# Four combinations on VectorE, moved in between the sums of the fourth weight piece

## The chip, the cores and the metric

The kernel runs on one core of one Trainium2 chip. The metric is the device time of one execution in microseconds (us). Five engines matter: TensorE (PE; PEld is its weight load), VectorE (DVE), ScalarE (ACT), GpSimd (POOL) and SyncE (SP), which issues most of the transfers (DMAs).

## The reference

The input `x` has the shape (32, 128, 2048). Two layers of the same form follow each other: `x = x + ffn(cond(x))`. Cut to what matters here, the first layer is

```python
out = einsum('boi,bih->boh', agg_w, x) + agg_b      # cond: one 128 x 128 mix for each batch
out = einsum('bsd,od->bso', out, W) + bias          # ffn: 2048 x 2048
xa  = einsum('bsd,erd->ebsr', out, A)               # 16 low-rank updates of rank 16
upd = einsum('ebsr,eor,e->bso', xa, Bf, coeffs * scales)
```

The second layer is a grouped convolution with 9 taps, and an up and a down projection with a GELU between them on permuted columns.

The 16 low-rank updates have together the rank 256, so the kernel folds them into the weights: W' = W^T + A^T diag(coeffs x scales) B^T. W' is 2048 x 2048; A and B^T have 256 rows, which are two halves of 128 (called `c` in the code).

## The kernel before

**The large product.** `x` times W' is computed by Strassen's scheme on two levels. The outer level has seven rounds (`ROUNDS`: P1, P2, P6, P7, P5, P3, P4), and each round runs over NG = 8 groups of four batches. `multiply` does one group of one round; it holds the seven inner products, each of four matmuls of 128 x 128 by 128 x 512 (L332). The inner combinations of the weights are made on GpSimd by `inner_weights` (L239 to L243), those of `x` by `x_combine` (L296 to L299). The second layer's work is put between the products of the last round, and the two projections (L676, L687) end the kernel.

**Building W'.** W' is made in 16 blocks (`blocks`), each of four pieces of 128 x 512, with two indices kh and oh for the quarter and kc for the place in it. The first four blocks (kh = oh = 0) are made directly by `w_make`, one after the other: for each piece two matmuls over the two halves `c` (L172), into a bank of PSUM, and a sum on VectorE that adds the bank to W^T's piece in SBUF (L176). The other twelve blocks are made two at a time by `w_make_two`, in front of each of the first six groups of the first round. That function uses Strassen's scheme too: seven products of one matmul for each block (L210), each followed on VectorE by a sum into a piece of W' (L213). P1, P6, P7 and P4 of a block accumulate in one bank, and the sum behind each of them reads it, so the next of them waits for that sum. The products take combinations of A's columns (`a_combine`, on GpSimd, L184 to L187) and of B^T's columns (`b_combine`): four subtractions of 128 x 512 (L196 to L199), the second of which uses the first and the fourth the second. `tb[1]` serves the blocks with oh = 1 and is made on VectorE; `tb[0]` is made on GpSimd in a later group. P1 and P2 need no combination of B^T, P6 needs the second.

**The order.** The order of instructions on each engine is written out by hand: it is that in which the Python code calls them (`manual_schedule`), and each engine takes its own instructions in that order. Buffers come from one pool of 24 slots (`slot`), and eight banks of PSUM go round in a queue (`bank`, `done`). The opening order is: loads of A, of B^T for oh = 0, of the first blocks of W^T; then of B^T for oh = 1 (`b_load(1, q)`, L141, into `bf_sb[1]`) and of the fifth and sixth block (L156); `a_combine(0)`; the four direct blocks by `make_first` from within `inner_weights`; `b_combine(1)`; then the loop over the steps, whose first iteration issues `w_make_two` for the fifth and sixth block and then `multiply`. `make_first` also adds a piece of each block to `wsum` on GpSimd (L870), the sums over W' from which a later bias is made.

In `b_combine` the four source pieces are those of the two halves and two column groups:

```python
b11, b12, b21, b22 = (bf_sb[oh][:, c, oi] for c in range(2) for oi in range(2))
```

Of the kernel before, what the change touches and what calls it, by code (L numbers as in the profile page):

```python
# [11 lines left out]
ALU = mybir.AluOpType  # L12
# [39 lines left out]
def adaln_ffn_kernel(  # L52
# [16 lines left out]
    nc = tc.nc  # L69
# [8 lines left out]
    def slot(name, shape=(P, L)):  # L78
        return big.tile(list(shape), FP, name=name, tag="s")


    def bank():
        return banks.pop(0)

    def done(*ps):
        banks.extend(ps)
# [39 lines left out]
    def a_load(h, k0, k1):  # L126
        for ki in range(2):
            i0 = (2 * h + ki) * QW
            nc.sync.dma_start(
                a_sb[h][:, :, ki, k0:k1].rearrange("p c k i -> p c (k i)"),  # L130
                A[:, :, i0 + k0 * P : i0 + k1 * P],
            )
# [26 lines left out]
    def w_store(k, t):  # L159
        nc.gpsimd.dma_start(wb_d[k], t.rearrange("p k o c -> p (k o c)"))  # L160

    def w_make(k, t):

        kh, oh, kc = k
        for oi in range(2):
            for ki in range(2):
                pw = bank()

                n = QW // 2 if k == (0, 0, 0) and oi == 0 else QW
                for o0 in range(0, QW, n):  # L170
                    for c in range(2):
                        nc.tensor.matmul(  # L172
                            pw[:, o0 : o0 + n], lhsT=a_sb[kh][:, c, ki, kc],
                            rhs=bf_sb[oh][:, c, oi, o0 : o0 + n], start=(c == 0), stop=(c == 1),
                        )
                nc.vector.tensor_tensor(t[:, ki, oi], pw, t[:, ki, oi], ALU.add)  # L176
                done(pw)
        w_store(k, t)


# [12 lines left out]
    def b_combine(oh, tt):  # L193
        t = slot(f"tb_{oh}", (P, 4, QW))
        b11, b12, b21, b22 = (bf_sb[oh][:, c, oi] for c in range(2) for oi in range(2))
        tt(t[:, 0], b12, b11, ALU.subtract)  # L196
        tt(t[:, 1], b22, t[:, 0], ALU.subtract)
        tt(t[:, 2], b22, b12, ALU.subtract)
        tt(t[:, 3], b21, t[:, 1], ALU.subtract)  # L199
        return {  # L200
            "P1": b11, "P2": b21, "P3": b22, "P4": t[:, 3],
            "P5": t[:, 0], "P6": t[:, 1], "P7": t[:, 2],
        }
# [67 lines left out]
    def x_loads(r, g):  # L271
        return {
            "P1": lambda: [x_load(g, 0, 0)],
            "P2": lambda: [x_load(g, 0, 1)],
            "P6": lambda: [x_load(g, 1, 0), x_load(g, 1, 1), x_load(g, 0, 0)],
            "P7": lambda: [x_load(g, 0, 0), x_load(g, 1, 0)],
            "P5": lambda: [x_load(g, 1, 0), x_load(g, 1, 1)],
            "P4": lambda: [x_load(g, 1, 1)],
            "P3": lambda: [x_load(g, 0, 1), part_load("s2", g)],
        }[r]()  # L280

    def x_combine(r, g, ts):

        a = ts[0]
        tt = nc.gpsimd.tensor_tensor
        if r == "P6":

            b, a, c = ts
            pieces(b, b, a, ALU.add)
            pieces(a, b, c, ALU.subtract)  # L290
            part_store("s2", g, a)
        if r in ("P7", "P5", "P3"):
            pieces(a, a, ts[1], ALU.add if r == "P5" else ALU.subtract)
        s = slot(f"s_{r}{g}", (P, 4, QW))
        a11, a12, a21, a22 = a[:, 0, 0], a[:, 1, 0], a[:, 0, 1], a[:, 1, 1]
        tt(s[:, 0], a21, a22, ALU.add)  # L296
        tt(s[:, 1], s[:, 0], a11, ALU.subtract)
        tt(s[:, 2], a11, a21, ALU.subtract)
        tt(s[:, 3], a12, s[:, 1], ALU.subtract)  # L299
        return {  # L300
            "P1": a11, "P2": a12, "P3": s[:, 3], "P4": a22,
            "P5": s[:, 0], "P6": s[:, 1], "P7": s[:, 2],
        }
# [412 lines left out]
    def small():  # L716
# [120 lines left out]
    blocks = [  # L837
        (kh, oh, kc) for kh, oh in ((0, 0), (0, 1), (1, 1), (1, 0)) for kc in range(4)
    ]
# [20 lines left out]
    lhs, sa, tb = {}, {}, {}  # L860
    sa[0] = a_combine(0, nc.gpsimd.tensor_tensor)
    first = [wt.pop(k) for k in blocks[0:4]]

    def make_first(kc):
        t = first[kc]
        w_make(blocks[kc], t)
        made.append(blocks[kc])
        if kc == 2:
            lhs[0] = x_combine(*steps[0], xs.pop(0))
        nc.gpsimd.tensor_tensor(wsum[:, 0, 1], wsum[:, 0, 1], t[:, 0, 1], ALU.add)  # L870

    rhs = inner_weights("P1", first, make_first)
    tb[1] = b_combine(1, nc.vector.tensor_tensor)
    a_load(1, 0, 4)
    unsummed, unsummed_first = [], list(first)
    olds = {}
# [4 lines left out]
    def olds_load(i):  # L881
        r, g = steps[i]
        olds[i] = [old and part_load(old, g) for old, _ in ADDED[r]]

    for i, (r, g) in enumerate(steps):
        ri = i // NG
        last_round = ri + 1 == len(ROUNDS)
        if i + 1 < len(steps):
            if i + 1 not in xs:
                xs[i + 1] = x_loads(*steps[i + 1])  # L890
            if not last_round:
                lhs[i + 1] = x_combine(*steps[i + 1], xs.pop(i + 1))
        if i + 2 < len(steps) and ri > 0 and not last_round:
            xs[i + 2] = x_loads(*steps[i + 2])
        if i == 0:
            olds_load(0)
        if i + 1 < len(steps) and not last_round:
            olds_load(i + 1)
        if g == NG - (1 if ri else 2) and ri < len(ROUNDS) - 1:
            nxt = inner_weights(ROUNDS[ri + 1], [nxt[kc] for kc in range(4)])  # L900

        if ri == 0:
            ks = blocks[4 + 2 * g : 6 + 2 * g]
            if ks:
                two = [wt.pop(k) for k in ks]
                w_make_two(ks, two, sa[ks[0][0]], tb[ks[0][1]])
                made.extend(ks)
                if g == 1:
                    a_scale(1, 0, 4)
                    sa[1] = a_combine(1, nc.gpsimd.tensor_tensor)  # L910
                if g == 3:
                    tb[0] = b_combine(0, nc.gpsimd.tensor_tensor)
                for k, t in zip(ks, two):
                    unsummed.append((k[1], t))
                    if k[:2] == (1, 0):
                        nxt[k[2]] = t
        elif ri + 1 < len(ROUNDS):
            for k, combine in waiting.items():
                nxt[k] = combine()
            waiting = {}  # L920
            if 2 <= g < 6:
                waiting[g - 2] = outer_weights(ROUNDS[ri + 1], g - 2)

        if last_round and g == 0:
            late_loads()
        if last_round and g == 2:

            late["te"] = mix.rearrange("p (k r) c -> p k r c", k=2)
            nc.sync.dma_start(mix.rearrange("p k c -> p (k c)"), te_d)
        k0 = 3 * (g - NG)  # L930
        if last_round:
            stage(k0, stage_first)

        def between(j):
            b = (ri - 1) * (NG - 2) + g
            if ri > 0 and g < NG - 2 and b < B and j < KEXP // 2:
                mixed_kernel(b, (2 * j, 2 * j + 1))
            if ri == 0 and j == 2:
                for k in blocks[6 + 2 * g : 8 + 2 * g]:
                    wt[k] = w_load(*k)  # L940
            if ri == 0 and j in (1, 3) and unsummed:
                row_sums(*unsummed.pop())
            if ri == 0 and j == 5 and unsummed_first:
                t = unsummed_first.pop(0)
                tt = nc.vector.tensor_tensor
                tt(wsum[:, 0, 0], wsum[:, 0, 0], t[:, 0, 0], ALU.add)
                tt(wsum[:, 0], wsum[:, 0], t[:, 1], ALU.add)
            if last_round:
                if j == 3 and i + 1 < len(steps):
                    lhs[i + 1] = x_combine(*steps[i + 1], xs.pop(i + 1))  # L950
                    olds_load(i + 1)
                if j in (2, 4):
                    stage(k0 + j // 2, stage_first)
                if j % 2:
                    stage_third(k0 + j // 2)
                else:
                    stage(k0 + j // 2, stage_second)

        multiply(r, g, lhs.pop(i), rhs, olds.pop(i), between)
        next(chain, None)  # L960
        if last_round and g >= 6:
            pair(g - 6)
        if last_round and g == 7:
            rings()
            gather_two(0)
        if g == NG - 1 and ri + 1 < len(ROUNDS):
            rhs = nxt
            nxt = {}

    before = None  # L970
    for k, (g, h) in enumerate(heads):
# [5 lines left out]
        t = ts.pop(k)  # L977
# [75 lines left out]
```

## Time and profile before

| what | value |
|---|---|
| median of 3 runs | 2651.13 us (2650.91 to 2654.36) |
| the profiled execution, its own time | 2649.93 us |
| its span (first to last instruction) | 2648.2 us |
| TensorE busy in the span | 2620.2 us, 99% |
| VectorE busy | 1335.3 us, 50% |
| GpSimd busy | 1200.2 us, 45% |
| ScalarE busy | 535.2 us, 20% |
| TensorE's products of L210, share of the chain that ended last | 2% |
| TensorE's products of L332, share of that chain | 49% |

The times of the profile are microseconds from the start of the span. A group of instructions is named by its line, its engine, its operation and its tiles, with buffer numbers left out. "PE bank L210 <- DVE w L213" reads: TensorE's instruction of L210, which writes a bank, waited for VectorE's instruction of L213, which writes `w`. A float32 matmul appears as two records. Busy shares of an engine that is not the bound say little: what counts is which wait ends last at a place.

### The profile page before, as it was taken

What the parts mean: (1) busy time and instruction counts of PE and PEld (TensorE: products, weight loads), DVE (VectorE), ACT (ScalarE), POOL (GpSimd) and SP (SyncE); (2) the same over time, 40 slices, a digit from 0 to 9 for tenths busy, and PEclk for the clock granted to TensorE, in tenths of its full rate; (3) what the DMA queues carried; (4) which work ended last, traced back from release to release, by engine and by line L of the source; (5) the groups of instructions that cost most, each with busy time, mean ns of one, the idle gap of its engine ahead of it and who ended that gap; (6) DMA issues with size and microseconds to landing.
All of it is one profiled execution on the core that took longest, in us unless ns stands there. A gap on an engine that the chain in (4) does not pass through costs nothing.

```text
span 2648.2 us, 20100 instructions
## 1 busy us (share of the span) xinstructions
PE 2620.2 (99%) x6484; PEld 1234.3 (47%) x6484; DVE 1335.3 (50%) x2168; ACT 535.2 (20%) x1103; POOL 1200.2 (45%) x950
## 2 busy tenths in 40 slices
PE   9999999999999999999999999999999999999998
PEld 4444444444444444444444445555455544555543
DVE  5554134343233454433366666666666666666610
ACT  0000000000000000000011144444444444444432
POOL 7321536978756644756332333333433333333222
PEclk9999999999999999999999999999999999999999
DMA  8542458688466577565657788777678777777532
GB/s 317 201 163 103 163 194 325 266 327 351 153 247 254 221 284 288 222 256 201 226 203 240 221 304 283 234 220 232 228 248 255 224 227 227 239 240 237 164 126 88
DMA packets 183609, 609.18 MB, mean 230 GB/s; under 512 B 16848, under 2 KB 88016, under 8 KB 139088
## 3 DMA queue, kind: packets, MB, share of 16 engines
q1 hardware_dynamic: 150080, 474.79, 50.8%
q0 software_dynamic: 32992, 132.14, 14.5%
q8 instruction: 52, 0.85, 0.1%
q10 hardware_dynamic: 432, 0.96, 0.1%
q14 instruction: 53, 0.43, 0.0%
HBM read 372.42 MB, written 201.85 MB: 217 GB/s over the span
## 4 chain that ended last, share of the span: by engine, by line
PE 95%; DVE 2%; DMA 1%; issue 1%; SPq 0%; ACT 0%; POOLq 0%; DVEq 0%; ACTq 0%
PE bank L332 49%; PE bank L676 16%; PE bank L687 16%; PE bank L534 6%; PE bank L444 4%; PE bank L210 2%; PE bank L172 1%; DMA xg<-x 1%; DVE va L514 0%; DVE vb L513 0%; DVE vb L516 0%; DMA ws<-in_ffw 0%; DVE va L515 0%; DVE va L517 0%; DMA bf_sb<-in_BfT 0%
## 5 line engine op out<-in xcount | busy, mean ns | idle before, releaser
L676 PE MATMUL bank<-t,ws 128*128 128x512 f32 x1024 | 460.7, 593 | 1.0 <-DVE u L325 0.5
L687 PE MATMUL bank<-gl,ws 128*128 128x512 f32 x1024 | 460.2, 592 | 0.0
L694 POOL DMA_INDIRECT out<-t,orow x128 | 151.7, 1185 | 562.3 <-DVE t L692 493.8
L325 DVE TENSOR_TENSOR u<-bank,u 128x512 f32<-128x512 f32 x280 | 187.6, 688 | 418.0 <-PE bank L332 411.0
L679 ACT ACTIVATE gl<-bank 128x512 f32<-128x512 f32 x512 | 306.0, 598 | 447.3 <-PE bank L676 445.1
L332 PE MATMUL bank<-P_t,s_P 128*128 128x512 f32 x896 | 393.7, 592 | 0.0
L687 PEld LDWEIGHTS bank<-gl,ws 128*128 128x128 f32 x1024 | 194.8, 190 | 232.7 <-issue 230.8
L676 PEld LDWEIGHTS bank<-t,ws 128*128 128x128 f32 x1024 | 194.6, 190 | 228.0 <-issue 219.2
L332 PE MATMUL bank<-wo_P,s_P 128*128 128x512 f32 x640 | 283.1, 595 | 1.5 <-DVE u L325 1.5
L332 PE MATMUL bank<-wo_P,xt 128*128 128x512 f32 x640 | 281.5, 592 | 0.0
L332 PEld LDWEIGHTS bank<-P_t,s_P 128*128 128x128 f32 x896 | 170.5, 190 | 213.2 <-issue 211.2
L435 ACT ACTIVATE bank<-w,aggb 128x512 f32<-128x512 f32 x128 | 80.8, 684 | 890.2 <-DVE ags L406 872.6
L427 POOL TENSOR_TENSOR x<-x,fb 128x1024 f32<-128x1024 f32 x64 | 155.5, 2448 | 226.1 <-DMA x<-in_x 176.1
L692 DVE TENSOR_TENSOR t<-bank,t 128x512 f32<-128x512 f32 x128 | 87.9, 687 | 318.0 <-PE bank L687 318.0
L269 POOL TENSOR_TENSOR xt<-xt,xt 128x512 f32<-128x512 f32 x128 | 159.6, 1280 | 157.7 <-DMA xt<-in_xT 157.7
L332 PE MATMUL bank<-P_t,xt 128*128 128x512 f32 x448 | 201.5, 593 | 0.0
L325 DVE TENSOR_TENSOR p<-bank,p 128x512 f32<-128x512 f32 x112 | 77.5, 692 | 238.8 <-PE bank L332 238.8
L296 POOL TENSOR_TENSOR s_P<-xt 128x512 f32<-128x512 f32 x56 | 71.8, 1283 | 272.1 <-DMA xt<-in_xT 215.8
L332 PEld LDWEIGHTS bank<-wo_P,s_P 128*128 128x128 f32 x640 | 122.3, 191 | 154.2 <-issue 152.5
L332 PEld LDWEIGHTS bank<-wo_P,xt 128*128 128x128 f32 x640 | 121.7, 190 | 152.1 <-issue 150.1
L406 DVE SCALAR_TENSOR_TENSOR ags<-mix,att_bc,ags 128x128 f32<-128x128 f32 x224 | 155.9, 696 | 4.5
L660 POOL DMA_INDIRECT t<-hx_d,row x128 | 124.8, 975 | 59.9 <-issue 24.7
(144 smaller groups left out, 2649.6 us busy)
## 6 DMA issues: line engine op xcount, KB each, us to landing
xt<-in_xT SPq DMA_DIRECT2D x88, 1024.0 KB, 8.9
u<-u_d SPq DMA_DIRECT2D x40, 1024.0 KB, 11.3
wo_P<-wb_d SPq DMA_DIRECT2D x36, 1024.0 KB, 14.2
u<-c_d SPq DMA_DIRECT2D x64, 512.0 KB, 5.9
x<-in_x SPq DMA_DIRECT2D x32, 1024.0 KB, 8.0
xg<-x SPq DMA_DIRECT2D x256, 128.0 KB, 5.6
hx_d<-x1t SPq DMA_DIRECT2D x32, 1024.0 KB, 5.3
hx_d<-ht SPq DMA_DIRECT2D x32, 1024.0 KB, 7.0
```

Of the source, the lines that this page charges most:

```text
L269: nc.gpsimd.tensor_tensor(out[:, i, j], a[:, i, j], b[:, i, j], op)
L325: nc.vector.tensor_tensor(to, ps, to, ALU.add)
L332: nc.tensor.matmul(ps, lhsT=lhs[k][:, bass.ts(kc, P)], rhs=rhs[k][kc], start=first and kc == 0, stop=last and kc == 3, skip_group_check=True,)
L406: nc.vector.scalar_tensor_tensor(ag, mix[:, k], att, ag, ALU.mult, ALU.add)
L427: nc.gpsimd.tensor_tensor(xt[:, f : f + 2], xt[:, f : f + 2], late["fb"][:, f : f + 2], ALU.add)
L444: nc.tensor.matmul(pm, lhsT=ag, rhs=u[:, f], start=False, stop=True, skip_group_check=True)
L534: nc.tensor.matmul(out, lhsT=w[:, 2 * i + r], rhs=rhs, start=first and r == 0, stop=last and r == 1, skip_group_check=True,)
L660: nc.gpsimd.indirect_dma_start(out=t.rearrange("p k t -> p (k t)"), out_offset=None, in_=hx_d[g].rearrange("l k t -> l (k t)"), in_offset= ...
L676: nc.tensor.matmul(pu, lhsT=w[:, m * P : (m + 1) * P], rhs=t[:, 0], start=True, stop=True)
L679: nc.scalar.activation(gl[m], pu, AF.Gelu)
L687: nc.tensor.matmul(pd, lhsT=w[:, (MC + m) * P : (MC + m + 1) * P], rhs=gl[m], start=(m == 0), stop=(m == MC - 1),)
L694: nc.gpsimd.indirect_dma_start(out=out, out_offset=bass.IndirectOffsetOnAxis(ap=orow[:, g, h : h + 1], axis=0), in_=t[:, 1], in_offset=None,)
```

## The change

`b_combine` no longer issues its four subtractions. It allocates their buffer, and returns a function `part`, each call of which issues the next of the four, together with the table of operands. `w_make` takes a function `between` and calls it after each of its four sums; by default it does nothing. For the fourth direct block `make_first` hands it `part` of `b_combine(1)`, so VectorE gets sum, combination, sum, combination, sum, combination, sum, combination in place of four sums and then four combinations. The buffer for `tb[1]` is allocated ahead of `inner_weights` instead of behind it. For `tb[0]` the four calls of `part` stand in a loop at the old place.

```diff
-    def w_make(k, t):
+    def w_make(k, t, between=lambda: None):
...
                 nc.vector.tensor_tensor(t[:, ki, oi], pw, t[:, ki, oi], ALU.add)
                 done(pw)
+                between()
         w_store(k, t)
...
     def b_combine(oh, tt):
         t = slot(f"tb_{oh}", (P, 4, QW))
         b11, b12, b21, b22 = (bf_sb[oh][:, c, oi] for c in range(2) for oi in range(2))
-        tt(t[:, 0], b12, b11, ALU.subtract)
-        tt(t[:, 1], b22, t[:, 0], ALU.subtract)
-        tt(t[:, 2], b22, b12, ALU.subtract)
-        tt(t[:, 3], b21, t[:, 1], ALU.subtract)
-        return {
+        parts = [
+            (t[:, 0], b12, b11), (t[:, 1], b22, t[:, 0]), (t[:, 2], b22, b12), (t[:, 3], b21, t[:, 1])
+        ]
+
+        def part():
+            if parts:
+                tt(*parts.pop(0), ALU.subtract)
+
+        return part, {
             "P1": b11, "P2": b21, "P3": b22, "P4": t[:, 3],
             "P5": t[:, 0], "P6": t[:, 1], "P7": t[:, 2],
         }
...
     first = [wt.pop(k) for k in blocks[0:4]]
 
+    part, tb[1] = b_combine(1, nc.vector.tensor_tensor)
+
     def make_first(kc):
         t = first[kc]
-        w_make(blocks[kc], t)
+
+        if kc == 3:
+            w_make(blocks[kc], t, part)
+        else:
+            w_make(blocks[kc], t)
         made.append(blocks[kc])
...
     rhs = inner_weights("P1", first, make_first)
-    tb[1] = b_combine(1, nc.vector.tensor_tensor)
     a_load(1, 0, 4)
...
                 if g == 3:
-                    tb[0] = b_combine(0, nc.gpsimd.tensor_tensor)
+                    part, tb[0] = b_combine(0, nc.gpsimd.tensor_tensor)
+                    for _ in range(4):
+                        part()
```

## The prediction

> **What bounds the kernel now.** I read the busy shares first, then TensorE's waits in the opening stage, then the engines' own timelines around the longest of them.
>
> ```profile
> PE 2620.2 (99%) x6484; PEld 1234.3 (47%) x6484; DVE 1335.3 (50%) x2168; ACT 535.2 (20%) x1103; POOL 1200.2 (45%) x950
> PE bank L210 <- DVE w L213: 4.0, 1, 4.0
> ```
>
> TensorE is busy for all but 28 us of 2648.2 us, so only what shortens its idle time or its slow clock can move the end. The second line (waits of the first 62 us: who waited for whom, us in total, times, longest) is the longest single wait of the whole run: one wait of 4.0 us, in which TensorE stands before the products of L210 until VectorE has added a sum of L213. TensorE's timeline shows where (start, length, records; in brackets the idle time before):
>
> ```profile
> 35.51 3.60 PE L210 MATMUL bank<-bf_sb,a_sb 128*128 128x512 f32 x8
> 43.09 7.08 PE L210 MATMUL bank<-tb,sa 128*128 128x512 f32 x12 [3.98 <-DVE w L213]
> 50.01 1.88 PE L210 MATMUL bank<-bf_sb,sa 128*128 128x512 f32 x4
> ```
>
> One product here is two records, 0.43 us each at full clock (the four from 50.01 are followed at 51.73). The eight from 35.51 are P1 and P2 for the two weight blocks; the product P6 of the first block is then due at 38.95 and starts at 43.09. VectorE in the same time:
>
> ```profile
> 33.99 0.69 DVE L176 TENSOR_TENSOR w<-bank,w 128x512 f32<-128x512 f32 x1 [1.02 <-PE bank L172]
> 35.71 0.69 DVE L176 TENSOR_TENSOR w<-bank,w 128x512 f32<-128x512 f32 x1 [1.03 <-PE bank L172]
> 36.32 1.01 DVE L196 TENSOR_TENSOR tb<-bf_sb 128x512 f32<-128x512 f32 x1
> 37.37 1.64 DVE L197 TENSOR_TENSOR tb<-bf_sb,tb 128x512 f32<-128x512 f32 x1
> 38.93 1.75 DVE L198 TENSOR_TENSOR tb<-bf_sb 128x512 f32<-128x512 f32 x1
> 40.59 1.75 DVE L199 TENSOR_TENSOR tb<-bf_sb,tb 128x512 f32<-128x512 f32 x1
> 42.26 1.87 DVE L213 TENSOR_TENSOR w<-bank,w 128x512 f32<-128x512 f32 x3
> ```
>
> Four sums of the fourth direct piece, each with 1.03 us idle before it (30.56, 32.28, 33.99, 35.71), then the four combinations in 5.94 us, and only then P1's first sum, at 42.26, for which P6 waits since both use one bank. The combinations are slow: a two-input operation of this size took 0.68 us (L946) while GpSimd stood still, these take up to 1.75. GpSimd's timeline shows the partner:
>
> ```profile
> 36.74 1.71 POOL L870 TENSOR_TENSOR wsum<-wsum,w 128x512 f32<-128x512 f32 x1
> 38.41 1.71 POOL L239 TENSOR_TENSOR P_t<-w 128x512 f32<-128x512 f32 x1
> 40.20 1.59 POOL L240 TENSOR_TENSOR P_t<-w,P_t 128x512 f32<-128x512 f32 x1
> ```
>
> Each combination ends 0.55 us after the GpSimd operation it overlaps (L870 ends 38.45, L197 39.01; L239 40.12, L198 40.68), and each GpSimd operation 1.11 us after the combination before it: they take turns, 1.67 us a pair.
>
> The wait costs more than its length. Windows of the same stretch (length, PE, PEld, DVE, ACT, POOL busy, then granted clock):
>
> ```profile
> 40.30:43.80 3.50, 0.71 (x2) 0.49 (x3) 3.50 (x5) 0.00 (x0) 3.42 (x3) 1.00 1.06 427
> 43.80:47.20 3.40, 3.40 (x5) 1.35 (x4) 2.23 (x4) 0.00 (x0) 3.30 (x4) 0.51 1.01 422
> 47.20:50.60 3.40, 3.40 (x9) 1.49 (x8) 2.46 (x4) 0.00 (x0) 3.32 (x4) 0.99 0.99 417
> ```
>
> For one stretch of 3.4 us after the gap TensorE ran at half clock, which loses 0.5 x 3.4 = 1.7 us. So the place costs 4.1 us idle (38.95 to 43.09) and 1.7 us of clock.
>
> [...] the combinations and their GpSimd partners take turns as above, and the sums of L176, with one input in PSUM, took 0.69 us beside GpSimd operations of 1.27. [...]
>
> **The change part by part.** The order of instructions of the two programs differs on VectorE alone: the same four combinations now stand after the first, second, third and fourth sum of L176. No instruction, transfer or buffer wait is added or removed; the other edit, for tb[0], issues the same four GpSimd operations at the same place and costs nothing. Naively the 0.61 us of work in each combination fits into the 1.03 us holes and the whole 4.1 us would go. Two things stand against that.
>
> First, the data. The first combination needs the second half of B^T for oh = 1 (L141), and now asks for it at 31.2 instead of 36.3:
>
> ```profile
> 12.15 0.55 SPq L141 DMA_DIRECT2D bf_sb<-in_BfT  x1
> DMA to landing us min/median/max: 21.1/21.1/21.1
> 15.68 0.33 SPq L156 DMA_DIRECT2D w<-in_WT  x1
> w<-in_WT SPq DMA_DIRECT2D x1, 1024.0 KB, 25.0
> ```
>
> It lands at 12.15 + 21.1 = 33.25. Until then VectorE stands, and behind it the sums of 32.28 and later. Second, the turns with GpSimd, now L297 (33.06 to 34.32), L298, L299, L870. My run of VectorE: combination 1 starts 33.3, ends 0.55 after L297, 34.87; sum 2 to 35.5; combination 2 ends with the next turn, 36.54; sum 3; combination 3, 38.21; sum 4; combination 4, 39.88. P1's first sum then starts at 39.80 (it started 0.08 before the end of L199) against 42.26: **2.46 us earlier**. Its weight block landed at 13.18 + 23.1 = 36.3, and its product is ready at 36.4. P6 follows 0.83 us after the start (42.26 to 43.09), at 40.63. P2's second product needs the bank of sum 2 at 38.09, which is free from 35.5; no new wait.
>
> P1's second sum needs the second block (last two lines above): 15.68 + 25.0 = 40.68. So it runs 40.75 to 41.44, and P6's second product starts at 41.58, 0.09 later than its place behind the first. This is a cap too: if the turns cost nothing, P6's second product could still not start before 41.58. **Gap: 2.46 - 0.09 = 2.4 us gained**, whichever of the two limits holds.
>
> Clock: TensorE is now idle from 38.95 to 40.63, 1.7 us[...]. Elsewhere in this trace 1.29 us of idle time before L534 at 1915.68 left the clock full, and 1.41 + 1.47 us close together before 1443.77 dropped it, as did 3.80 at 1384.58. [...] I take no drop: **1.7 us gained**; the bounds are 0 and 1.7.
>
> GpSimd gets its four waits two operations earlier, and about 0.2 us more in sum; it ends L243 at 54.1 now and TensorE uses that (P7 of the first multiply) only at 67.2, after the change near 63: hidden, 8 us of slack. Everything after follows from TensorE's progress: the next weight blocks landed by 53 and are used from 77 on, so the loads stay covered when that becomes 73.
>
> Sum: 2.4 + 1.7 = 4.1 us. The profiled execution took 2649.93 (span 2648.2, 1.7 around it), and would become 2645.8. The median before, 2651.13, lies 1.2 above it, so 2647.0 for the median.
>
> **The rivals.** (A) *The clock drops all the same*[...]: only the gap's 2.4, 2648.7. For it: the threshold is not shown; against: the 1.29 us case. (B) *The landing is earlier or the turns cheaper than thought, and nearly the whole place goes*: 5.8 us, 2645.3, just past the limit of "faster". Against: both landings would have to come 2 us earlier, while the DMA engines are full (shares of 1.0 in the windows above) with the same list of loads. (C) *Slower: late turns between VectorE and GpSimd fall worse.* The place is conv_inputs (L513 to L518) in the last round, where [...] TensorE waited 3.80 before L534, with a half-clock stretch behind it: 3.8 + 1.7 = 5.5 us for one such meeting. The early shift moves GpSimd's phase against loads there. One more such meeting gives 2651.1 - 4.1 + 5.5 = 2652.5, two give 2658; it decides from 4.1 us of added waits on. For it: one of the three runs lies 3.2 us above the others. Against: GpSimd's work there is released by transfers that follow TensorE's progress and shift with it. (D) *It does nothing*, if the landing at 33.25 were past 35.7: P6 would start no earlier than now. The margin is 2.4 us; 2651.
>
> **How the numbers follow.** 0.2% is 5.3 us, about what a measurement of this kernel can tell from no change. Forecast 60% (2647.0); A 15%, D 7%, both within 0.2%; B 10%, of which half or a little more passes the limit; C 8%, of which most is more than one meeting. Run-to-run scatter puts some tenth of the forecast's share past the limit on the fast side, which with B's share gives faster 0.14; C's larger cases give slower 0.05; the rest, 0.81, is within. The range reaches from B's side, with a little scatter, 2644.9, over A to just short of no gain, 2650.5.
>
> **What would show it.** The first combination waits for in_BfT until about 33.3; combinations of 1.6 us; P1's first sum near 39.8; TensorE's wait before tb 1.5 instead of 3.98; clock 1.00 after it; L332's first product at 49.3 instead of 53.44. I am wrong if the gap is under 0.8 or over 2.5, if the clock halves, or if L332 starts 4 us earlier and the end does not.

## The result, and the profile after

The changed kernel took 2646.71 us (median of 19 runs, 2642.03 to 2652.69) beside 2650.91 us for the kernel before (19 runs, 2647.77 to 2655.53): a ratio of 0.9983, 95% interval 0.9976 to 0.9989. That is 4.2 us, between 2.9 and 6.4. In a second comparison of the same two kernels (`after_again`) it was 2.9 us: 2647.81 us over 13 runs beside 2650.70, a ratio of 0.9988 (0.9979 to 0.9996).

The profiled execution took 2644.05 us, its span is 2642.2. Behind the change `b_combine` issues at L203, `w_make_two` is at L215 and L218, `multiply` at L337, and GpSimd's lines have moved by five to eleven (L299 to L304, L870 to L881, L239 to L244).

Before, one wait of 4.0 us stood out in the first 62 us. Now these two stand in its place (who waited for whom, us in total, times, longest):

```profile
DVE tb L203 <- DMA bf_sb<-in_BfT: 0.7, 1, 0.7
PE bank L215 <- DVE w L218: 0.3, 1, 0.3
```

The wait of TensorE is nearly gone, and a new one has appeared on VectorE, for B^T. TensorE's timeline (start, length, records, idle before):

```profile
36.42 3.60 PE L215 MATMUL bank<-bf_sb,a_sb 128*128 128x512 f32 x8
40.32 5.39 PE L215 MATMUL bank<-tb,sa 128*128 128x512 f32 x12 [0.30 <-DVE w L218]
45.54 1.88 PE L215 MATMUL bank<-bf_sb,sa 128*128 128x512 f32 x4
```

P6 starts at 40.32 and its twelve records take 5.39 us instead of 7.08. VectorE's timeline shows the new order, and what it waits for:

```profile
31.47 0.69 DVE L176 TENSOR_TENSOR w<-bank,w 128x512 f32<-128x512 f32 x1 [1.02 <-PE bank L172]
32.82 1.71 DVE L203 TENSOR_TENSOR tb<-bf_sb 128x512 f32<-128x512 f32 x1 [0.66 <-DMA bf_sb<-in_BfT]
34.45 0.68 DVE L176 TENSOR_TENSOR w<-bank,w 128x512 f32<-128x512 f32 x1
35.05 1.16 DVE L203 TENSOR_TENSOR tb<-bf_sb,tb 128x512 f32<-128x512 f32 x1
36.13 0.68 DVE L176 TENSOR_TENSOR w<-bank,w 128x512 f32<-128x512 f32 x1
36.73 1.16 DVE L203 TENSOR_TENSOR tb<-bf_sb 128x512 f32<-128x512 f32 x1
37.81 0.68 DVE L176 TENSOR_TENSOR w<-bank,w 128x512 f32<-128x512 f32 x1
38.41 1.16 DVE L203 TENSOR_TENSOR tb<-bf_sb,tb 128x512 f32<-128x512 f32 x1
39.49 4.37 DVE L218 TENSOR_TENSOR w<-bank,w 128x512 f32<-128x512 f32 x7
```

The first combination waits for the load, and from there VectorE works without a hole: each pair of a sum and a combination takes 1.68 us. GpSimd beside it (three of its operations):

```profile
33.94 1.72 POOL L303 TENSOR_TENSOR s_P<-xt 128x512 f32<-128x512 f32 x1
35.62 1.73 POOL L304 TENSOR_TENSOR s_P<-xt,s_P 128x512 f32<-128x512 f32 x1
40.78 1.28 POOL L245 TENSOR_TENSOR P_t<-w,P_t 128x512 f32<-128x512 f32 x1
```

Its operations take 1.72 and 1.73 us while the combinations run and 1.28 behind them: the turns are still paid, in another place. Last, the windows of the same stretch (length, PE, PEld, DVE, ACT, POOL busy, then granted clock):

```profile
40.30:43.80 3.50, 3.48 (x8) 1.61 (x9) 3.50 (x6) 0.00 (x0) 3.34 (x4) 1.00 1.04 423
43.80:47.20 3.40, 3.40 (x9) 1.52 (x8) 2.73 (x5) 0.00 (x0) 3.30 (x4) 1.00 1.01 417
```

The granted clock is 1.00 where it was 0.51 before.

The two profiled spans differ by 6.0 us, more than the medians. 4.46 of it is there when L332's (now L337's) first product starts, 53.44 before and 48.98 now. The rest is in the last round. Before, TensorE stood idle there for 1.41 and 1.47 us, and a stretch at half clock followed that this execution of the changed kernel does not have (first line before, second after):

```profile
1443.40:1446.60 3.20, 2.83 (x4) 1.31 (x5) 3.20 (x7) 0.00 (x0) 0.00 (x0) 0.50 0.79 267
```

```profile
1439.30:1442.60 3.30, 3.30 (x10) 1.60 (x9) 3.30 (x8) 0.00 (x0) 0.00 (x0) 1.00 1.12 299
```

From 1350 to 1460 us the mean granted clock was 0.97 in the profile before, and 0.98 and 0.97 in the first two of the changed kernel; in the third it was 1.00 from 1430 to 1450. Whether the change makes such a stretch rarer is not shown.

### The profile page after: what moved, and what is told of

It reads as the page before. It is cut to its first block, busy times and chain, and to the rows that moved or that the text cites. A ratio compares the mean times of both kernels' runs of the same rounds, so it can differ in the third digit from the quotient of the medians.

```text
span 2642.2 us, 20100 instructions
## 1 busy us (share of the span) xinstructions
PE 2616.9 (99%) x6484; PEld 1231.8 (47%) x6484; DVE 1334.7 (51%) x2168; ACT 535.8 (20%) x1103; POOL 1202.6 (46%) x950
## 4 chain that ended last, share of the span: by engine, by line
PE 94%; DVE 3%; DMA 2%; issue 0%; SPq 0%; POOLq 0%; ACT 0%; DVEq 0%; ACTq 0%
PE bank L337 50%; PE bank L681 16%; PE bank L692 16%; PE bank L539 6%; PE bank L449 4%; PE bank L215 2%; DMA bf_sb<-in_BfT 1%; DMA xg<-x 1%; DVE va L519 1%; DVE vb L518 1%; DVE vb L521 0%; DMA ws<-in_ffw 0%; DVE va L520 0%; DMA a_sb<-in_A 0%; DVE va L522 0%
## 5 line engine op out<-in xcount | busy, mean ns | idle before, releaser
L337 PE MATMUL bank<-P_t,s_P 128*128 128x512 f32 x896 | 393.7, 592 | 0.0
L337 PE MATMUL bank<-wo_P,s_P 128*128 128x512 f32 x640 | 281.6, 592 | 1.5 <-DVE u L330 1.5
L337 PE MATMUL bank<-wo_P,xt 128*128 128x512 f32 x640 | 281.5, 592 | 0.0
L337 PEld LDWEIGHTS bank<-P_t,s_P 128*128 128x128 f32 x896 | 170.2, 190 | 213.4 <-issue 211.4
L337 PE MATMUL bank<-P_t,xt 128*128 128x512 f32 x448 | 201.4, 592 | 0.0
L337 PEld LDWEIGHTS bank<-wo_P,s_P 128*128 128x128 f32 x640 | 121.5, 190 | 153.6 <-issue 152.0
L337 PEld LDWEIGHTS bank<-wo_P,xt 128*128 128x128 f32 x640 | 121.6, 190 | 152.2 <-issue 150.2
```

The lines of the kernel that those rows point to most:

```text
L337: nc.tensor.matmul(ps, lhsT=lhs[k][:, bass.ts(kc, P)], rhs=rhs[k][kc], start=first and kc == 0, stop=last and kc == 3, skip_group_check=True,)
```

## The experiments

Twelve executions can be set side by side by four times of TensorE: its first product of L172, which waits for the first load of B^T; P6's start and the idle time before it; and L332's first product. "Front" is the last less the first, "rest" is from L332's first product to the end of the span. All in us, lines by the numbers of before.

| kernel | first L172 | idle before P6 | P6 | first L332 | front | rest |
|---|---|---|---|---|---|---|
| before | 6.22 | 3.98 | 43.09 | 53.44 | 47.2 | 2594.8 |
| before, 2nd profile (`before_again`) | 7.16 | 4.54 | 44.72 | 55.08 | 47.9 | 2595.9 |
| changed | 7.17 | 0.30 | 40.32 | 48.98 | 41.8 | 2593.2 |
| changed, 2nd (`after_again`) | 6.60 | 1.51 | 41.06 | 49.72 | 43.1 | 2597.6 |
| changed, 3rd (`after_third`) | 7.23 | 0.44 | 40.52 | 49.17 | 41.9 | 2594.4 |
| buffer alone (`e8_slot`) | 6.54 | 3.92 | 43.62 | 53.98 | 47.4 | 2594.3 |
| gap filled (`e1_fill`) | 6.81 | 0.58 | 43.72 | 52.38 | 45.6 | 2595.1 |
| no turns (`e2_noturns`) | 6.52 | 0, then 0.73 | 39.26 | 48.84 | 42.3 | 2595.9 |
| B^T late, new order (`e3_late`) | 6.41 | 3.04 | 46.13 | 54.79 | 48.4 | 2596.2 |
| B^T late, old order (`e5_late_before`) | 7.02 | 3.77 | 48.92 | 57.58 | 50.6 | 2595.1 |
| loads earlier, new order (`e4_early`) | 6.00 | 0.64 | 38.56 | 47.22 | 41.2 | 2595.7 |
| loads earlier, old order (`e7_early_before`) | 7.48 | 5.78 | 46.10 | 56.43 | 49.0 | 2594.3 |

**The clock alone.** To the kernel before, four matmuls that nothing reads:

```diff
         product("P2", pzs, True, True, 0, 0)
+        if ks[0] == blocks[4]:
+            for _ in range(4):
+                nc.tensor.matmul(
+                    banks[0], lhsT=a_sb[0][:, 0, 0, 0], rhs=bf_sb[0][:, 0, 0], start=True, stop=True
+                )
         done(*pzs)
```

> The kernel before, with four more matmuls of 128 x 128 by 128 x 512 on a free bank between P2 and P6 of the first pair of Strassen pieces; nothing reads them. They fill about 3.4 us of the gap, and VectorE's order is that of before, so P6 still waits for P1's first sum and starts near 43.1. Theory (the gain has two parts, 2.4 us of gap and 1.7 us of clock): the granted clock stays 1.00 behind the gap, and the stretch from P6's start to the first product of L332 is 8.6 us, as in the changed kernel, instead of 10.35; the first product of L332 near 51.7. Rival (the clock's part comes from something else, such as the adds that now run ahead): the stretch stays near 10.3.

TensorE's timeline of this kernel, with the filling matmuls in its first line, and then a window of it (the granted clock is the third number from the end):

```profile
39.54 3.60 PE L219 MATMUL bank<-bf_sb,a_sb 128*128 128x512 f32 x8
43.72 5.39 PE L210 MATMUL bank<-tb,sa 128*128 128x512 f32 x12 [0.58 <-DVE w L213]
```

```profile
43.80:47.20 3.40, 3.40 (x8) 1.52 (x9) 3.39 (x6) 0.00 (x0) 3.24 (x4) 1.00 1.01 422
```

P6 is as late as in the old order, and yet the clock behind it is 1.00, its records take 5.39 us, and L332's first product follows 8.66 us later (52.38 less 43.72), as in all three profiles of the changed kernel; in the three profiles of the old order at that place it is 10.35 or 10.36. So 1.7 us of the gain are the clock's, and to get them it is enough to keep TensorE busy. This is one profile; its single run, 2649.30 us beside a median of 2651.09, says little by itself.

**The turns, and the second limit.** From the changed kernel, with that part of the computation left out which the expectation names:

```diff
+            tt = nc.gpsimd.tensor_tensor
+            if name == "P1" and kc == 2:
+                tt = lambda o, a, b, op: nc.gpsimd.memset(o, 0.0)
             tt(t1[:, kc], b12, b11, ALU.subtract)
...
+        if (r, g) == steps[0]:
+            tt = lambda o, a, b, op: nc.gpsimd.memset(o, 0.0)
         tt(s[:, 0], a21, a22, ALU.add)
...
-        nc.gpsimd.tensor_tensor(wsum[:, 0, 1], wsum[:, 0, 1], t[:, 0, 1], ALU.add)
+        if kc != 2:
+            nc.gpsimd.tensor_tensor(wsum[:, 0, 1], wsum[:, 0, 1], t[:, 0, 1], ALU.add)
```

> The changed kernel, with the GpSimd operations that read SBUF beside the combinations turned into writes alone: x_combine of the first step and the combinations of the third direct block in inner_weights are memsets, and the third block's piece isn't added to wsum. That part of the computation is left out. Theory (turns with GpSimd's reads stretch the combinations, the load of B^T holds the first): the first combination still waits for in_BfT until about 33, but each takes about 0.6 to 0.7 us instead of 1.16 to 1.7; P1's first sum near 37.1 instead of 39.5. P6 of the first block then starts without a wait, and its second product waits for the sum that needs the sixth weight block, near 41.5: the first product of L332 comes no more than 0.5 us earlier than in the changed kernel. Rival (no second limit): L332's first product 1.4 us earlier than in the changed kernel, where TensorE's start is equal.

VectorE's timeline of this kernel (four of its lines):

```profile
32.87 0.69 DVE L203 TENSOR_TENSOR tb<-bf_sb 128x512 f32<-128x512 f32 x1 [1.30 <-DMA bf_sb<-in_BfT]
35.28 0.68 DVE L203 TENSOR_TENSOR tb<-bf_sb 128x512 f32<-128x512 f32 x1
37.23 0.68 DVE L218 TENSOR_TENSOR w<-bank,w 128x512 f32<-128x512 f32 x1
40.26 1.29 DVE L218 TENSOR_TENSOR w<-bank,w 128x512 f32<-128x512 f32 x2 [2.35 <-DMA w<-in_WT]
```

With GpSimd at memsets, which read nothing, or waiting, the combinations take 0.68 and 0.69 us, and P1's first sum comes at 37.23, 2.3 us earlier than in the first profile of the changed kernel. The first product of L332 comes 0.14 us earlier, with a start of TensorE that is 0.65 earlier: P1's second sum stands 2.35 us for the sixth weight block. Both limits are as forecast, and they lie so close that taking one away alone brings almost nothing; the single run took 2646.50 us, as the changed kernel does.

**The load as the bound.** The same edit to the changed kernel (`e3_late`) and to the kernel before (`e5_late_before`):

```diff
-    for q in range(2):
-        b_load(1, q)
     for k in blocks[4:6]:
         wt[k] = w_load(*k)
+    for q in range(2):
+        b_load(1, q)
```

> The changed kernel, with the loads of B^T for oh = 1 issued behind those of the fifth and sixth weight block (2 MB more in front of them, about 5 us at the 420 GB/s of this stretch). Theory (what counts is when the second half of B^T lands, then four turns of 1.67 us): it lands near 38.2, the first combination ends near 39.3, P1's first sum comes near 44.3, P6 near 45.2, and TensorE also waits before P2's second product for the bank of the second sum. The clock drops again. L332's first product near 55.5, so about 2 us slower than the kernel before, 6 slower than the changed one, and equal within 0.6 us to the same load order with the old order of VectorE. Rival (the order alone makes the gain): 4 us faster than the latter.

> The kernel before, with the loads of B^T for oh = 1 issued behind those of the fifth and sixth weight block. Theory: the first combination waits for the load until about 38.2 instead of starting at 36.3, the four end near 44.4, P6 starts near 45.2, clock at half for a window behind it; L332's first product near 55.5, about 2 us slower than before. Rival (the load plays no part in the old order): as before, 53.4.

The first combination waited for its load until 40.6 and 41.0, not until 38.2. The new order took 2652.72 us (20 runs), a ratio of 1.0006 to the kernel before (0.9999 to 1.0013), and 6.0 us more than the changed kernel: that far a late load takes the gain away, as the theory has it. But the old order took 2658.50 us (7 runs), a ratio of 1.0028 (1.0016 to 1.0039): 7.4 us slower than before where I had about 2. So with equal loads the new order is 5.8 us faster by the medians, where the theory had at most 0.6 and the rival 4. The theory missed here. In the two profiles P6 is 2.8 us earlier in the new order; the old order's profile is of one of the two shortest of its seven runs (2654.54 us), and where the rest of the 5.8 us arises is not shown. Of the 2.8 us 0.4 are the load's; the rest comes from the four turns, which did not fall as I had them. VectorE of the new order, and then GpSimd's wait beside it:

```profile
41.83 1.16 DVE L203 TENSOR_TENSOR tb<-bf_sb,tb 128x512 f32<-128x512 f32 x1
43.51 0.68 DVE L203 TENSOR_TENSOR tb<-bf_sb 128x512 f32<-128x512 f32 x1
```

```profile
45.09 0.56 POOL L160 DMA_DIRECT2D wb_d<-w  x1 [2.65 <-DVE w L176]
```

VectorE of the old order:

```profile
43.41 3.10 DVE L198 TENSOR_TENSOR tb<-bf_sb 128x512 f32<-128x512 f32 x1
```

In the new order the fourth block's last sum is held up with the combinations, GpSimd waits for that sum and has nothing left to read, and three of four combinations run at 0.69 us. In the old order GpSimd goes on (L870 at 43.46 for 1.27 us, L239 at 44.69 for 1.26), and one combination takes 3.10. The clock, too, did otherwise than forecast: in `e3_late` it was 1.00 from 37.45 to 51.10, and in `e5_late_before` it was 0.50 from 40.23 to 43.64, ahead of P6, while P1 and P2 ran, and 1.00 from there to 50.47 (last section).

**Both loads earlier.** The same two moves in the changed kernel (`e4_early`) and in the kernel before (`e7_early_before`), beside the changed kernel as it is (`after_again`):

```diff
-    xs = {0: [x_load(0, 0, 0)]}
     for k in blocks[2:4]:
...
     for k in blocks[4:6]:
         wt[k] = w_load(*k)
+    xs = {0: [x_load(0, 0, 0)]}
...
-        if kc == 2:
-            lhs[0] = x_combine(*steps[0], xs.pop(0))
...
     rhs = inner_weights("P1", first, make_first)
+    lhs[0] = x_combine(*steps[0], xs.pop(0))
```

> The changed kernel once more, beside the next two. Theory (two parts: 2.4 us of gap, 1.7 us of clock): about 4.1 us under the kernel before. From TensorE's first product of L172 to its first of L337 it took 41.8 us in the first profile of the changed kernel and 47.2 before; here 41.4 to 43, the more the earlier TensorE starts against the landing of the second half of B^T. No drop of the clock in the first 100 us. Rival (most of the 6.0 us by which the first two profiles' spans differ belongs to the change): 6 us under before.

> The changed kernel, with the first load of x^T issued behind those of B^T for oh = 1 and of the fifth and sixth weight block, which so have 1 MB less in front of them (about 2.4 us at 420 GB/s), and with x_combine of the first step behind inner_weights on GpSimd. Theory (two limits: the landing of B^T's second half, that of the sixth weight block): both land about 2.4 us earlier, near 30.5 and 38. The first combination waits for no load, P6 of both blocks starts without a wait, and from TensorE's first product of L172 to the first of L337 it takes 41.4 us, whatever TensorE's start; about 5.8 us under the kernel before and 0.4 to 1.6 under the changed one. Rival (only the turns with GpSimd hold the changed kernel back): a wait before P6 as in the changed kernel.

> The kernel before, with the same two moves as the kernel with the earlier loads (x^T's first load behind those of B^T and of the two weight blocks, x_combine of the first step behind inner_weights). Theory (in the old order the combinations wait for VectorE's sums and not for the load): no gain; P6 comes after the fourth combination as before, the clock drops, 47.2 us from the first product of L172 to the first of L332; within 1 us of before. Rival (the earlier load is worth the time by itself): 1.5 us or more under before.

`e4_early` has a median of 2645.59 us, a ratio of 0.9983 to the kernel before (0.9977 to 0.9990); `after_again` 2647.81 and 0.9988 (0.9979 to 0.9996). Both were timed beside the same runs of the kernel before, so they can be compared directly: `e4_early` is faster by 2.2 us in the medians and by 2.0 in the means of its 21 and the other's 13 runs (95% interval, worked out from these runs, 0.8 to 3.2). Against the gain of the first comparison, 4.2 us, its own of 5.1 is only 0.9 more, so the earlier loads are worth some 1 to 2 us. In the traces L332's first product is at 47.22 instead of 48.98 to 49.72. P6 still waits 0.64 us, which I had ruled out. VectorE's timeline of `e4_early`, and then GpSimd's:

```profile
31.95 2.51 DVE L203 TENSOR_TENSOR tb<-bf_sb,tb 128x512 f32<-128x512 f32 x1
```

```profile
31.40 1.28 POOL L879 TENSOR_TENSOR wsum<-wsum,w 128x512 f32<-128x512 f32 x1
32.63 1.27 POOL L244 TENSOR_TENSOR P_t<-w 128x512 f32<-128x512 f32 x1
```

The second combination, ready at 31.95, let two GpSimd operations pass. The turns are not strict; what decides them I have not settled. `e7_early_before` gained nothing (2651.79 us, 1.0002, 0.9994 to 1.0011): in the old order the load is not what the combinations wait for.

**The buffer alone.** To the changed kernel:

```diff
-        if kc == 3:
-            w_make(blocks[kc], t, part)
-        else:
-            w_make(blocks[kc], t)
+        w_make(blocks[kc], t)
...
     rhs = inner_weights("P1", first, make_first)
+    for _ in range(4):
+        part()
```

> One part of the change alone: the buffer of the combinations is allocated ahead of inner_weights, and the four combinations are issued behind the four sums, as in the kernel before. Theory (the order on VectorE makes the gain, the place of the buffer nothing): as before, with a wait of 4 us before P6, about 47.2 us from the first product of L172 to the first of L332 (here L337), and the time within 0.1% of before. Rival (the place of the buffer plays a part): faster by 2 us or more, or slower in the last round.

2650.93 us, ratio 1.0000 (0.9992 to 1.0009), and the old front:

```profile
43.62 7.08 PE L215 MATMUL bank<-tb,sa 128*128 128x512 f32 x12 [3.92 <-DVE w L218]
```

Within these limits the order on VectorE makes the whole gain.

**Is any of it given back?** Two more profiles:

> The kernel before, for a second profile. Theory: 47.2 us from the first product of L172 to the first of L332[...]; from there to the end 2593 to 2598 us as in the other profiles, whichever order VectorE has. Rival (the change gives back about 1 us in the last round): under 2595.2 again, where the kernels with the new order average 2595.7.

> The changed kernel, for a third profile. Theory: 41.8 to 43.1 us from the first product of L172 to the first of L337; from there to the end 2593 to 2598. Rival (about 1 us given back in the last round): over 2595.2.

Their single runs took 2652.76 and 2645.46 us. The rest is 2594.8, 2595.9 and 2594.3 in the three profiles with the old order unaltered otherwise (`e8_slot` is one), mean 2595.0; and 2593.2, 2597.6 and 2594.4 with the new one, mean 2595.1. It scatters by some 4 us and shows no shift that three profiles each could tell. Two differences cancel in it. TensorE's waits behind 60 us come to 12.6, 12.2 and 11.7 us with the old order, and to 12.6, 14.3 and 13.2 with the new one, 1.2 us more in the mean, most of it for `va` in the last round (the profile before, then the first of the changed kernel):

```profile
PE bank L534 <- DVE va L517: 7.8, 6, 3.8
PE bank L539 <- DVE va L522: 9.1, 7, 3.6
```

On the other side, two, three and two stretches of the last round ran at half clock with the old order, and one, two and one with the new one, at 1.7 us each; the mean granted clock of the whole executions was 0.997, 0.996 and 0.997, and 0.998 in each of the three with the new order. Whether either difference belongs to the change stays open. L332's first product comes 4.9 us earlier in the mean of three profiles each (54.17 and 49.29), somewhat more than the 4.2 and 2.9 us of the two comparisons; some of it may be given back in the last round, but this is not shown.

## Why the prediction was right

**The total.** 4.1 us forecast, 2647.0; measured 4.2, 2646.71. That the two agree to 0.1 us is in part luck: the interval is 2.9 to 6.4, the second comparison gave 2.9, and the terms below add up to 4.5 to 4.9 in the traces.

**The clock's term**, 1.7 us: 10.35 to 8.66 us from P6 to L332, shown by `e1_fill` apart from the rest. Rival A did not happen: behind the gap P6's twelve records take 5.39 us in all three profiles, as in `e1_fill` at a clock of 1.00. Only one of them, with a gap of 1.51 us, comes near the gap that A was about.

**The gap's term**, 2.4 us: P6 went from 43.09 to 40.32 in the first two profiles, 2.8, and from a mean of 43.81 to one of 40.63 in three each, 3.2. The term was somewhat low, because the old order's P6 moves with TensorE's start (36.9 to 37.6 us behind it), and the executions looked at later started later than the one I worked from. In the new order P6 is tied to the load: it starts 7.50 and 7.48 us behind the first combination's start in the first two profiles (32.82 and 33.58), where my steps gave 7.3.

**What I gave as a sign of being wrong came up.** A gap under 0.8 us: it was 0.30 and 0.44 in two profiles of three and 1.51 in the other. The step that failed is the time when P6 is due. I took TensorE's start from the profile of before, 6.22; in the two profiles with the short gap it was 7.17 and 7.23, so P6 was due 1 us later, while B^T's second half landed no later. At 6.60 the gap was the 1.5 forecast.

**The two limits.** The first combination waited for the load to 32.82, 33.58 and 33.13 (33.3 forecast). The sixth weight block as the cap behind it is shown by `e2_noturns`, and in the third profile of the changed kernel it is itself the last wait, by 0.2 us (VectorE's timeline):

```profile
40.57 1.89 DVE L218 TENSOR_TENSOR w<-bank,w 128x512 f32<-128x512 f32 x3 [0.20 <-DMA w<-in_WT]
```

**The other rivals.** B needed both loads 2 us earlier; `e4_early`, which gives them that, has the shortest front and is 1 to 2 us faster than the changed kernel. C, turns falling worse in the last round, did not come as a further meeting of 5.5 us; 1.2 us more of waits are there in the mean, and fewer stretches at half clock make up for them in these profiles. D, a later landing, is what `e3_late` makes; its landing is far past the 35.7 that I gave as the limit. Against the kernel before the gain is gone, but against the old order with the same loads it is not.

**GpSimd's cover** held: from 30 to 110 us of the three profiles of the changed kernel, which takes in P7 of the first `multiply`, TensorE's only wait is the one before P6, for VectorE.

## What to carry to other kernels

Holes of an engine are only worth what the moved work finds there: ask first when its operands land, and which engine reads beside it, and work the new order out to the instant. When two limits end within tenths of a microsecond of each other, taking one away shows nothing, so name the second before moving the first. And price an idle stretch of TensorE with the half clock behind it: here 1.7 us on top of 4, which filler matmuls alone saved in `e1_fill`. The price is not there each time: in `e3_late` gaps of 3.43 and 3.04 us left the clock at 1.00.

## What the runs showed of the hardware

**Where the clock fell.** In the profiles before and after, every change of the granted clock lies 3.413 us or a multiple of it behind the one ahead: before, half clock lasts from 43.857 to 47.270, and the next fall is at 1385.294, 392 times 3.413 us later. With the two traces cut into stretches of 3.413 us at these changes, the first 12 us left aside, TensorE's busy records in the stretch ahead of a fall came to 0.77, 0.71 and 1.13 us before and to 0.29 after, and to 1.22 and 1.25 ahead of the last fall, behind which no product follows. In every other stretch at full clock they came to 2.08 us or more before and 1.91 or more after, and full clock followed.

The two kernels with late loads have stretches between these figures. Cut at edges that I worked out from their clock's changes, which is an estimate for `e3_late`, whose clock did not change here (columns as above), `e3_late`:

```profile
37.45:40.86 3.41, 1.46 (x4) 0.77 (x5) 0.24 (x1) 0.00 (x0) 3.25 (x4) 1.00 1.04 379
40.86:44.27 3.41, 2.23 (x6) 0.59 (x4) 3.41 (x6) 0.00 (x0) 1.58 (x1) 1.00 1.02 418
```

and `e5_late_before`:

```profile
36.81:40.23 3.42, 1.30 (x3) 0.32 (x3) 0.69 (x1) 0.00 (x0) 3.34 (x4) 1.00 1.01 407
40.23:43.64 3.41, 3.41 (x5) 1.35 (x4) 2.58 (x3) 0.00 (x0) 3.31 (x4) 0.50 1.06 422
```

Behind 1.46 us of busy records the clock was 1.00, behind 1.30 it was 0.50. `e3_late` had gaps of 3.43 and 3.04 us at a clock of 1.00; in `e5_late_before` the fall came behind a gap of 2.12. How idle TensorE must be for a fall is not shown beyond these cases.

**How it came back.** Before, half clock lasted 3.413 us three times, with 3.41, 3.41 and 2.96 us of busy records in it, and after once, with 2.97; full clock followed each time. So I estimate a cost of up to 1.7 us for each of these falls, half of 3.413.

**The turns are not fair.** Three combinations took 2.51, 2.99 and 3.10 us, in `e4_early`, `e7_early_before` and `e5_late_before`, and beside each two GpSimd operations of 1.26 to 1.28 us ran instead of one. In the changed kernel's three profiles the longest took 1.71, 1.70 and 1.60.
